# A gated layer's activation: ScalarE's silu in place of its sigmoid and a VectorE product

## The chip, the cores and the metric

The kernel runs on one core of one Trainium2 chip. The metric is the device time of one execution in microseconds (us), the median of several runs. The core has a matrix engine (TensorE, PE in the profile, with its weight loads as PEld), a vector engine (VectorE, DVE), an activation engine (ScalarE, ACT), GpSimd (POOL), and SyncE (SP), which here only issues transfers. Matmul results land in PSUM, which has 8 banks of 128 x 512 fp32.

## The reference

Four layers run over `x` of 8 x 512 x 512 fp32, each as `x = x + layernorm(layer(layernorm(x)))`: a softmax attention of `x` with itself, a mixing by a sum of eight factors, a grouped-query attention, and a gated feed-forward layer. The last is the one that matters here:

```python
g = jnp.einsum('th,ih->ti', xf, gate_w) * gate_s
u = jnp.einsum('th,ih->ti', xf, up_w) * up_s
hdn = jax.nn.silu(g) * u
out = jnp.einsum('ti,hi->th', hdn, down_w) * down_s
```

The hidden size is 512 and the inner size 1408, which is 11 blocks of 128. `silu(g)` is `g * sigmoid(g)`. The weights `gate_w`, `up_w` and `down_w` hold only -1, 0 and 1.

## The kernel before

The kernel works through eight batches of 512 tokens, each held as four tiles of 128 tokens by 512. For each batch it runs four stages: `stage_attn0`, `stage_ffn0`, `stage_attn1` and `stage_ffn1`. They are not executed in the order of the code. Every operation is first recorded by `Recorder.add` (line 75) with its engine, an estimated duration, the buffers it reads and writes, and a priority. The priority comes from a table of due times by kind of step and batch (`DUE`, line 1285, and `due`, line 1348). After all operations of all batches are recorded, `Recorder.issue` (line 118) goes through an estimated time line. At each step it looks, for each engine, at the operations that are ready and for which buffers are free. Among those that can start within a small slack of the earliest it takes the one that is due first, and then issues the pick that starts earliest over all engines. Each engine executes its instructions in the order so found. One batch's softmax rows and layernorms thus come to lie between the matmuls of another batch. The estimates count a change of the activation table on ACT as 1.3 us, and changes between shapes of the matmul array on PE as 0.09 or 0.21 us.

Buffers are handed out in the same pass: a `row` buffer (18 of them) holds a 128 x 512 tile in SBUF, `f` is one of the eight PSUM banks, `wgu` one of four buffers for a block of gate or up weights, `hd0` and `hd1` hold the hidden activations of a batch, `hl` (two) the split operands of a matmul.

The last layer is `stage_ffn1`. Its matmuls run in a reduced fp32 format on operands that are split into a leading part and a rest (`in_parts`, line 1083: ACT writes the leading part at line 1094, DVE the rest at 1103). For each of the 11 blocks of the inner size it

- loads a block of gate weights and one of up weights by `load_slice`, on POOL's queue (line 382),
- multiplies the gate block with the tokens into bank `pg` and the up block into bank `pu`, 8 matmuls each (line 1160),
- applies the sigmoid on ACT with the per-row scale `gate_s` (line 1180), from `pg` into a `row` buffer `sig`,
- forms `pg * gate_s * sig` on DVE, in place in `sig` (line 1190),
- forms `pu * up_s * sig` on DVE into `hd` (line 1199).

When all blocks are there, the down matmuls (line 1228) multiply `hd` with the resident `wd`, and line 1249 scales the result and hands it to the layernorm and the residual sum (lines 511 to 554).

In all but the last batch a gate block covers the 512 tokens at once. In the last batch the first four blocks (`FEW`) are done for tokens 0 to 255 and then for 256 to 511, so that there are 92 gate products in all: 84 of 128 x 512 and 8 of 128 x 256.

Two readings of other lines are needed below. Line 575 is the softmax exponential, the only other function that needs a table of its own; its maxima are taken on DVE at line 568. Lines 608, 658, 865, 885, 900, 922, 982 and 1014 are copies and scalings on ACT that bring results out of PSUM.

The whole program is recorded twice, the second time in plain fp32 behind a condition that the data of this case does not meet. Line 240 reads the flag for it.

Of the kernel before, what the change touches and what calls it, by code (L numbers as in the profile page):

```python
# [13 lines left out]
AF = mybir.ActivationFunctionType  # L14
ALU = mybir.AluOpType
# [235 lines left out]
def layers(  # L251
# [23 lines left out]
    nc = tc.nc  # L275
# [67 lines left out]
    add = rec.add  # L343

    def when(kind, b, *steps):

        rec.prio = due(kind, b if b < B // 2 else b - B, B, *steps)
# [23 lines left out]
    gs = Fixed("gs", [P, NI])  # L371
# [124 lines left out]
    def ap(r):  # L496
        return r[1](buf_of(r).t)

    def whole(b):
        return (b, lambda t: t[:, :])  # L500
# [609 lines left out]
    def stage_ffn1(x, b, after):  # L1110
        PASS, array = (0.229, "128x128r") if split else (0.86, "128x128")
        xs = [Buf("hl") for _ in range(1 + split)]
        hds = [Buf(f"hd{c}") for c in range(len(CUTS))]


        every = tuple(range(NT))
        rounds, kind = [(every, range(NI))], "f1."
        if b in EARLY or b - B in EARLY:
            rounds = [((0, 1), range(FEW)), ((2, 3), range(FEW)), (every, range(FEW, NI))]
            kind = "h1."  # L1120
        known, products, rows = set(), [], []
        for q, (toks, its) in enumerate(rounds):
            cut = slice(toks[0] * P, (toks[-1] + 1) * P)
            mine = [(x_, (t, hf)) for x_ in xs for t in toks for hf in range(2)]
            took = (0.69, 0.75) if len(toks) == NT else (0.4, 0.42)
            for t in toks:
                if t in known:
                    continue
                known.add(t)
                when(kind + "norm", b, t - toks[0], q)  # L1130
                if t % 2 == 0:
                    pair = [Buf("row"), Buf("row")]
                xn = pair[t % 2]
                mv, rstd = moments(whole(x[t]))
                normalize(whole(xn), whole(x[t]), mv, rstd, room=[*xs, *pair])
                rows.append(whole(xn))
                if t % 2 == 0:
                    continue
                pts, into, bank = transpose_two(xs[0], t - 1, rows[-2:], room=xs, copy=False)
                for hf in range(2):  # L1140
                    dsts = [((x_, (t, hf)), into(hf)) for x_ in xs]
                    in_parts(dsts, lambda hf=hf, bank=bank: bank(hf), [pts[hf]], 0.6, also=(t - 1, hf))

            for c, (lo, hi) in enumerate(CUTS):
                for it in range(lo, hi):
                    if it not in its:
                        continue
                    when(kind + "gate", b, it, q)
                    sig = Buf("row")
                    hd = (hds[c], lambda tt, k=it - lo, cut=cut: tt[:, k, cut])  # L1150
                    pg, pu = Buf("f"), Buf("f")
                    wg = load_slice("wgu", gate_t, it, after=after)
                    wu = load_slice("wgu", up_t, it, after=after)

                    def product(bank, w, cut=cut):
                        def go():
                            n = 0
                            for kt in range(KT):
                                for d in xs:
                                    nc.tensor.matmul(  # L1160
                                        bank.t[:, cut],
                                        w.t[:, kt, :],
                                        d.t[:, kt, cut],
                                        start=(n == 0),
                                        stop=(n == KT * len(xs) - 1),
                                    )
                                    n += 1

                        return go


                    us = PASS * KT * len(xs) * len(toks) / NT
                    mm(pg, us, product(pg, wg), [wg, *mine], room=[hds[c]], state=array)
                    products.append(mm(pu, us, product(pu, wu), [wu, *mine], state=array))
                    gsc = lambda it=it: gs.t[:, it : it + 1]
                    usc = lambda it=it: us_.t[:, it : it + 1]
                    add(
                        "ACT",
                        took[0],
                        lambda sig=sig, pg=pg, gsc=gsc, cut=cut: nc.scalar.activation(  # L1180
                            sig.t[:, cut], pg.t[:, cut], AF.Sigmoid, scale=gsc()
                        ),
                        reads=[pg, gs],
                        writes=[sig],
                        state="sig",
                    )
                    add(
                        "DVE",
                        took[1],
                        lambda sig=sig, pg=pg, gsc=gsc, cut=cut: nc.vector.scalar_tensor_tensor(  # L1190
                            sig.t[:, cut], pg.t[:, cut], gsc(), sig.t[:, cut], ALU.mult, ALU.mult
                        ),
                        reads=[pg, gs],
                        writes=[sig],
                    )
                    add(
                        "DVE",
                        took[1],
                        lambda sig=sig, pu=pu, usc=usc, hd=hd, cut=cut: nc.vector.scalar_tensor_tensor(  # L1199
                            ap(hd), pu.t[:, cut], usc(), sig.t[:, cut], ALU.mult, ALU.mult  # L1200
                        ),
                        reads=[pu, us_, sig],
                        writes=[(hds[c], (it - lo, u)) for u in range(2) if 2 * u in toks],
                    )
        for t in range(NT):
            po = Buf("f")
            for c, (lo, hi) in enumerate(CUTS):
                when(kind + "down", b, t, c)
                n = hi - lo
                if split:  # L1210

                    hl = Buf("hl")
                    half_of = lambda k, hl=hl, n=n: (
                        (hl, k),
                        lambda tt, k=k, n=n: flat(tt)[:, k * KT * D // 2 :][
                            :, : n * P
                        ].rearrange("p (i q) -> p i q", q=P),
                    )
                    src = lambda c=c, t=t: hds[c].t[:, :, ts(t, P)]
                    in_parts([half_of(0), half_of(1)], src, [(hds[c], (k, t // 2)) for k in range(n)], 0.78)  # L1220
                    ops = [half_of(0), half_of(1)]
                else:
                    ops = [(hds[c], lambda tt, t=t: tt[:, :, ts(t, P)])]

                def down(ops=ops, po=po, lo=lo, hi=hi):
                    for it in range(lo, hi):
                        for k, o in enumerate(ops):
                            nc.tensor.matmul(  # L1228
                                po.t[:, :],
                                ap(o)[:, it - lo, :],  # L1230
                                wd.t[:, it, :],
                                start=(it == 0 and k == 0),
                                stop=(it == NI - 1 and k == len(ops) - 1),
                            )

                add(
                    "PE",
                    PASS * n * len(ops),
                    down,
                    reads=[*{buf_of(o): 0 for o in ops}, wd],  # L1240
                    writes=[po],
                    after=products,
                    state=array,
                )
            z = Buf("row")
            add(
                "DVE",
                0.69,
                lambda po=po, z=z: nc.vector.tensor_tensor(
                    z.t[:, :], po.t[:, :], ds_bc.t[:, :], ALU.mult  # L1250
                ),
                reads=[po, ds_bc],
                writes=[z],
            )
            add_layernorm(whole(x[t]), whole(z), last=b == B - 1)
            add(
                "SP",
                0.85,
                lambda t=t: nc.sync.dma_start(out[b, ts(t, P), :], x[t].t[:, :]),
                reads=[x[t]],  # L1260
            )
# [138 lines left out]
```

## Time and profile before

| what | us |
|---|---|
| time, median of 3 runs (lowest to highest) | 1484.42 (1483.66 to 1485.83) |
| span of the profiled execution, first to last instruction | 1482.8 |
| PE busy in it | 1441.2 |
| DVE busy | 1059.0 |
| ACT busy | 624.6 |
| POOL busy | 570.3 |
| sigmoid, line 1180: 92 instructions | 61.7 |
| product with the gate, line 1190: 92 instructions | 66.7 |
| product with the up part, line 1199: 92 instructions | 66.4 |
| activation table loads: 16 of 1.283 us | 20.5 |

A line of a group in the profile reads: line of the kernel, engine, operation, output and input by the program's names, partitions x elements, the count, then busy us and the mean ns of one, and last the engine's idle time just before these instructions with what ended most of it (`<-`). A line of a wait reads: who waited for whom, then us in total, how many times, and the longest. The slices cut the span in 40 equal parts; a digit is the busy share in tenths. Matmuls are pipelined, so that PE's busy time is not work at its peak rate.

### The profile page before, as it was taken

The numbers are of one execution on the slowest core, as the hardware profiler recorded it, in microseconds if no ns is written. First come the engines' busy times: TensorE is split into PE (matmuls) and PEld (weight loads), VectorE is DVE, ScalarE is ACT, GpSimd is POOL, SyncE is SP. The second block draws the span as 40 slices with busy tenths as digits, with TensorE's granted clock in tenths as the row PEclk, the third lists the DMA queues.
The fourth block names the chain that finished last, engine by engine and source line by source line (L and its number), as shares of the span: only waits on it lengthen the run. The fifth ranks groups of instructions, "written<-read, shape, count | busy, mean of one in ns | idle before, by whom it ended". The sixth has DMA issues, their size and how long they took to land.

```text
span 1482.8 us, 23191 instructions
## 1 busy us (share of the span) xinstructions
PE 1441.2 (97%) x8562; PEld 906.9 (61%) x8562; DVE 1059.0 (71%) x2227; ACT 624.6 (42%) x1396; POOL 570.3 (38%) x884
## 2 busy tenths in 40 slices
PE   5999999999999999999999999999999999999986
PEld 3545567665756567565675656656566565765675
DVE  6989875778558784777838777487774868658745
ACT  3217534732257222672227712376114751247321
POOL 7760452137501473006720167201761117600541
PEclk9999999999999999999999999999999999999999
DMA  9632145014500254002540035300442003510281
GB/s 332 186 90 96 45 87 97 26 40 100 107 25 20 43 112 87 29 16 50 114 79 29 23 80 100 64 23 29 105 80 51 30 23 78 111 25 23 60 165 35
DMA packets 156700, 108.06 MB, mean 73 GB/s; under 512 B 7072, under 2 KB 137120, under 8 KB 156576
## 3 DMA queue, kind: packets, MB, share of 16 engines
q0 software_dynamic: 98736, 51.13, 18.4%
q1 hardware_dynamic: 57840, 55.34, 12.1%
q8 instruction: 70, 1.15, 0.3%
q14 instruction: 54, 0.44, 0.1%
HBM read 98.06 MB, written 8.39 MB: 72 GB/s over the span
## 4 chain that ended last, share of the span: by engine, by line
PE 78%; POOL 9%; DVE 8%; issue 2%; DMA 2%; SPq 0%; ACT 0%; POOLq 0%; DVEq 0%; ACTq 0%
PE f L1160 18%; PE f L1228 9%; PE f L939 8%; PE f L1001 8%; PE f L910 7%; PE f L1027 7%; PE f L970 5%; PE f L741 4%; PE f L688 4%; POOL rstd L527 3%; DVE row L535 3%; PE f L719 2%; PE f L880 2%; PE f L891 2%; DVE st L511 2%
## 5 line engine op out<-in xcount | busy, mean ns | idle before, releaser
L1160 PE MATMUL f<-hl,wgu 128*128 128x512 f32 (+1 forms) x1472 | 347.8, 391 | 6.1 <-DMA wgu<-in_up_t 3.0
L520 POOL TENSOR_SCALAR ve<-mv 128x1 f32<-128x1 f32 x224 | 67.6, 302 | 724.3 <-DVE mv L516 711.7
L1160 PEld LDWEIGHTS f<-hl,wgu 128*128 128x128 f32 x1472 | 265.9, 188 | 71.7 <-issue 14.4
L575 ACT ACTIVATE row<-f,s 128x512 f32<-128x512 f32 x288 | 196.7, 696 | 34.6 <-DVE s L568 31.9
L568 DVE TENSOR_REDUCE s<-f 128x1 f32<-128x512 f32 x288 | 185.5, 683 | 30.3 <-PE f L939 18.5
L1228 PE MATMUL f<-wd,hl 128*128 128x512 f32 x704 | 185.4, 415 | 1.4 <-DVE hl L1103 1.4
L554 POOL TENSOR_TENSOR x<-x,row 128x512 f32<-128x512 f32 x120 | 156.1, 1305 | 67.0 <-DVE row L535 62.0
L1180 ACT ACTIVATE row<-f,gs 128x512 f32<-128x512 f32 (+1 forms) x92 | 61.7, 670 | 243.9 <-PE f L1160 239.6
L1228 PEld LDWEIGHTS f<-wd,hl 128*128 128x128 f32 x704 | 131.9, 188 | 45.5 <-issue 9.7
L592 DVE TENSOR_SCALAR row<-row,s 128x512 f32<-128x512 f32 x288 | 147.7, 517 | 8.6
L982 ACT COPY big<-f 128x512 f32<-128x512 f32 x256 | 134.8, 598 | 40.3 <-PE f L970 37.9
L527 POOL TENSOR_TENSOR rstd<-ve,mhalf 128x1 f32<-128x1 f32 x224 | 135.2, 606 | 16.5
L939 PE MATMUL f<-row,big 64*128 64x512 f32 x512 | 128.7, 610 | 0.0
L1190 DVE SCALAR_TENSOR_TENSOR row<-f,gs,row 128x512 f32<-128x512 f32 (+1 forms) x92 | 66.7, 725 | 79.0 <-ACT row L1180 79.0
L1001 PE MATMUL f<-big,row 128*64 128x256 f32 x1024 | 120.4, 383 | 0.0
L1199 DVE SCALAR_TENSOR_TENSOR hd<-f,us,row 128x512 f32<-128x512 f32 (+1 forms) x92 | 66.4, 722 | 73.7 <-PE f L1160 71.7
L910 PE MATMUL f<-big,row 128*128 128x512 f32 x256 | 117.1, 601 | 0.0
L719 PE MATMUL f<-big,big 128*128 128x512 f32 x256 | 114.6, 597 | 1.1 <-DVE row L535 1.1
L741 PE MATMUL f<-fsum,row 128*128 128x512 f32 x256 | 115.5, 594 | 0.2 <-ACT row L575 0.2
L1027 PE MATMUL f<-row,big 128*128 128x512 f32 x256 | 114.9, 599 | 0.0
L1001 PEld LDWEIGHTS f<-big,row 128*64 128x64 f32 x1024 | 69.5, 137 | 51.3 <-ACT big L982 15.3
L970 PEld LDWEIGHTS f<-ident,row 64*128 64x128 f32 x2048 | 73.4, 139 | 40.6 <-issue 20.4
(84 smaller groups left out, 1849.2 us busy)
## 6 DMA issues: line engine op xcount, KB each, us to landing
wgu<-in_gate_t POOLq DMA_DIRECT2D x92, 256.0 KB, 3.5
wgu<-in_up_t POOLq DMA_DIRECT2D x92, 256.0 KB, 3.4
x<-in_x SPq DMA_DIRECT2D x32, 256.0 KB, 2.7
row<-in_wq_t SPq DMA_DIRECT2D x32, 256.0 KB, 5.0
row<-in_wo_t SPq DMA_DIRECT2D x32, 256.0 KB, 3.1
out<-x SPq DMA_DIRECT2D x32, 256.0 KB, 2.0
hd<-in_factors SPq DMA_DIRECT2D x28, 256.0 KB, 4.9
wd<-in_down_t POOLq DMA_DIRECT2D x11, 256.0 KB, 8.6
```

Source lines behind the costliest of these rows:

```text
L527: lambda: nc.gpsimd.tensor_tensor(rstd.t[:, :], ve.t[:, :], mhalf, ALU.pow),
L554: lambda: on.tensor_tensor(ap(xt), ap(xt), y.t[:, :], ALU.add),
L568: lambda: nc.vector.tensor_reduce(nmax.t[:, :], sc.t[:, :], AX.X, ALU.max, negate=True),
L575: lambda: nc.scalar.activation(e.t[:, :], sc.t[:, :], AF.Exp, bias=nmax.t[:, :], accum_out=tot.t[:, :]),
L592: lambda: nc.vector.tensor_scalar(e.t[:, :], e.t[:, :], rtot.t[:, :], None, ALU.mult),
L741: nc.tensor.matmul(po.t[:, :], xnT.t[:, ts(kt, P)], fsum.t[:, kt, :], start=(kt == 0), stop=(kt == KT - 1),)
L910: nc.tensor.matmul(pq.t[:, :], wq.t[:, ts(kt, P)], hT.t[:, kt, :], start=(kt == 0), stop=(kt == KT - 1),)
L939: nc.tensor.matmul(scs[g].t[:, :], qT.t[gp, i, ts(s, P)], kT.t[gp, :], start=True, stop=True,)
L1001: nc.tensor.matmul(po.t[gp, : 2 * P], v.t[:, t * P + g * DH : t * P + (g + 1) * DH], columns_of(aT)[:, g * NT + t, :], start=(t == 0), sto ...
L1027: nc.tensor.matmul(po.t[:, :], qT.t[:, i, ts(t, P)], wos[i].t[:, :], start=(i == 0), stop=(i == NPAIR - 1),)
L1160: nc.tensor.matmul(bank.t[:, cut], w.t[:, kt, :], d.t[:, kt, cut], start=(n == 0), stop=(n == KT * len(xs) - 1),)
L1228: nc.tensor.matmul(po.t[:, :], ap(o)[:, it - lo, :], wd.t[:, it, :], start=(it == 0 and k == 0), stop=(it == NI - 1 and k == len(ops) - 1),)
```

## The change

The activation on ACT becomes `Silu` with the same operands, the same estimated duration and the same table state `"sig"` for the planner. The DVE operation at line 1190 is no longer recorded. Line 1199 reads `sig` as before; what it reads there is now written by ACT alone. Bank `pg` has one reader less. Nothing else differs in the source: the estimates, due times and buffers stay.

```diff
@@ -1178,20 +1178,11 @@
                         "ACT",
                         took[0],
                         lambda sig=sig, pg=pg, gsc=gsc, cut=cut: nc.scalar.activation(
-                            sig.t[:, cut], pg.t[:, cut], AF.Sigmoid, scale=gsc()
+                            sig.t[:, cut], pg.t[:, cut], AF.Silu, scale=gsc()
                         ),
                         reads=[pg, gs],
                         writes=[sig],
                         state="sig",
-                    )
-                    add(
-                        "DVE",
-                        took[1],
-                        lambda sig=sig, pg=pg, gsc=gsc, cut=cut: nc.vector.scalar_tensor_tensor(
-                            sig.t[:, cut], pg.t[:, cut], gsc(), sig.t[:, cut], ALU.mult, ALU.mult
-                        ),
-                        reads=[pg, gs],
-                        writes=[sig],
                     )
                     add(
                         "DVE",
```

## The prediction

> **What bounds the kernel now.** I read the profile's totals and slices first, then the stretches of time, then what TensorE (PE) waited for, and last the instructions of the changed lines.
>
> ```profile
> span 1482.8 us, 23191 instructions
> ...
> PE 1441.2 (97%) x8562; PEld 906.9 (61%) x8562; DVE 1059.0 (71%) x2227; ACT 624.6 (42%) x1396; POOL 570.3 (38%) x884
> ...
> PE   5999999999999999999999999999999999999986
> ```
>
> PE is busy 1441.2 of 1482.8 us. Only 41.6 us exist in which it does nothing, whatever the other engines do. The stretches (start:end, length, busy time of each engine) show where those 41.6 us lie:
>
> ```profile
> 0.00:50.00 50.00, 33.74 (x180) 18.94 (x181) 35.40 (x72) 13.90 (x30) 34.22 (x60) 1.00 0.99 322
> 50.00:93.00 43.00, 38.92 (x185) 19.95 (x184) 39.53 (x84) 11.43 (x31) 33.86 (x50) 1.00 0.33 92
> 93.00:205.00 112.00, 110.91 (x732) 59.71 (x732) 100.59 (x220) 55.58 (x138) 42.35 (x62) 0.98 0.30 85
> ...
> 385.00:565.00 180.00, 179.57 (x1069) 113.02 (x1068) 127.14 (x273) 78.19 (x175) 67.72 (x107) 1.00 0.27 59
> ...
> 1395.00:1424.00 29.00, 23.96 (x158) 18.81 (x157) 18.76 (x37) 6.72 (x13) 16.21 (x24) 1.00 0.68 129
> ```
>
> The start costs 16.3 + 4.1 + 1.1 = 21.5 us, and the first instruction of a changed line comes at 213.3 us, so that part stays. A batch in the middle (about 180 us) leaves PE idle for 0.43 us. From 1395 to 1424 us it is idle for 5.0 us, later for 1.6 us more, and 10 us of layernorm and store follow its last matmul. VectorE (DVE) is 71% busy and no bound: 127 of 180 us in a middle batch. What PE waited for, with total us, times, longest:
>
> ```profile
> PE f L1160 <- DMA wgu<-in_up_t: 3.0, 3, 1.5
> ...
> PE f L604 <- DVE row L535: 2.3, 8, 0.6
> ...
> PE f L719 <- DVE row L535: 1.1, 5, 0.2
> PE f L1160 <- DMA wgu<-in_gate_t: 1.1, 2, 0.8
> PE f L1160 <- DVE row L1190: 0.8, 1, 0.8
> ```
>
> The product that is removed, L1190, held PE up once, for 0.8 us. The others here are weights that land late (4.1 us) and normalized rows that come late (3.4 us).
>
> **The change part by part.** The three groups of the gate (busy us, mean ns, then the engine's idle time before them):
>
> ```profile
> L1180 ACT ACTIVATE row<-f,gs 128x512 f32<-128x512 f32 (+1 forms) x92 | 61.7, 670 | 243.9 <-PE f L1160 239.6
> ...
> L1190 DVE SCALAR_TENSOR_TENSOR row<-f,gs,row 128x512 f32<-128x512 f32 (+1 forms) x92 | 66.7, 725 | 79.0 <-ACT row L1180 79.0
> ...
> L1199 DVE SCALAR_TENSOR_TENSOR hd<-f,us,row 128x512 f32<-128x512 f32 (+1 forms) x92 | 66.4, 722 | 73.7 <-PE f L1160 71.7
> ```
>
> *The product removed.* 92 instructions at 725 ns are 66.7 us of DVE, 8.2 us in a middle batch (11 at 750 ns). On the path to the end they are worth almost nothing, which the last product of the last batch shows, all engines in order of time (start, us, engine, line):
>
> ```profile
> 1447.92 2.43 PE L1160 MATMUL f<-hl,wgu 128*128 128x512 f32 x10
> ...
> 1448.57 0.69 ACT L1180 ACTIVATE row<-f,gs 128x512 f32<-128x512 f32 x1 [2.94 <-PE f L1160]
> ...
> 1449.29 0.75 DVE L1190 SCALAR_TENSOR_TENSOR row<-f,gs,row 128x512 f32<-128x512 f32 x1 [1.79 <-ACT row L1180]
> ...
> 1450.38 0.75 DVE L1199 SCALAR_TENSOR_TENSOR hd<-f,us,row 128x512 f32<-128x512 f32 x1 [0.34 <-PE f L1160]
> ```
>
> L1190 ends at 1450.04, and L1199 starts only at 1450.38, when PE has finished the up product. The up matmuls (8 at some 0.227 us, 1.81 us) cover the sigmoid (0.69) and L1190 (0.75) with 0.34 us over. Without L1190 the cover is about 1.1 us and L1199 still starts when the up product ends: 0 us. If that cover were gone, 0.75 us would be saved once per product, 66.7 us of DVE at most, and still not of PE.
>
> *The wait.* L1199 waits for ScalarE (ACT) directly. DVE's 79.0 us of idle time before L1190 moves in front of L1199, where PE ends it. Queued behind L1199 are softmax maxima (L568) and layernorm steps (L511, L535) of the other batch; they are not held longer, because L1199 itself is released by the same event as before. The queue of loads for the weights (POOL) and SP's stores are issued on releases by PE and POOL; none of these instructions is moved.
>
> *The bank of the gate product* is released by ACT's end instead of L1190's, 0.8 us earlier (1449.26 against 1450.04). That takes away the wait of 0.8 us at 1410 us. The products around it wait 0.7 to 1.5 us each for weights, so I count half: -0.4 us, bounds 0 and -0.8.
>
> *DVE work that comes earlier.* PE's waits for L535 total 3.4 us in the two rows above, 0.1 to 0.6 us each. With DVE lighter some vanish: bounds 0 and -3.4, taken -0.5, since these waits lie mostly after a layernorm chain through POOL and not behind an L1190.
>
> *The function.* Silu isn't in the trace. The nearest row is the sigmoid with the same operands, 689 ns for 128x512; the plain copy of that size takes 598 (L982) and the exponential 696 plus 209 for its accumulator. Bounds 598 to 905 ns, -8.4 to +19.9 us of ACT over 92 instructions. I take 689: +0. ACT is 78 of 180 us busy in a middle batch; even 905 ns ends about 0.9 us before the up product. 0 us on the path, at both ends.
>
> *Table loads.* There are 8 in front of the sigmoid, 7 in front of the exponential:
>
> ```profile
> L1180 ACT ACT_TABLE_LOAD x8 | 10.3, 1283 | 24.0 <-issue 18.6 <-PE f L1160 5.4
> L575 ACT ACT_TABLE_LOAD x7 | 9.0, 1283 | 5.6 <-DVE s L568 5.6
> ```
>
> Copies run between sigmoids without a load. If silu's table serves copies too, the count stays at 16 and the price is 0. If not, each change costs a load of 1.28 us; copies break into the run of sigmoids some 4 times in a middle batch, 8 loads more, 10 us of ACT, which has 100 us free there.
> The Trainium skill ("ScalarE: Activation LUTs", What ACT_TABLE_LOAD costs) speaks against mixing functions: it puts a switch at 2.66 us, drain included. Here the sigmoid follows a load of 1.283 us by 0.02 us (212.04 + 1.28, next start 213.34). By the skill's figure those 8 would be 21 us of ACT in a batch instead of 10, an estimate; either is hidden. The same page, Table sets, says that cheap functions such as copy are in every set, by which the count would not change at all; no run here shows that yet.
>
> *The order.* Every engine's order is computed from estimated durations, and with 92 entries gone from DVE's line it is computed anew. Up to about 212 us nothing differs; after that any decision may. The trace has no row for the new order, so I bound it by stretches of the old one. From 205 to 1395 us PE is idle for 3.6 us (0.3%), read from seven such stretches. Below: all of that gone, -3.6. Above: a stretch that is not the repeating pattern, 93 to 205 us, idles 1.09 of 112 us, 1.0%; over 1190 us that is 11.6 us, so +8.0. PE's order of array shapes matters as well: the same 8 matmuls of L910 take 3.44 us on the chain behind L891's and 3.63 us behind the 64-row ones of L939, 0.2 us for a change of shape. I counted 55 such changes between kinds in a middle batch, so one more or less in each is 0.2 x 6.6 batches = 1.3 us. I take +2.0, nearer to the repeating rows, since the work is the same and DVE, which feeds PE, is lighter.
>
> *Sum.* -0.4 - 0.5 + 0 + 0 + 2.0 = +1.1 us. The profiled execution has a span of 1482.8 us; the median of the three runs is 1484.42, 1.6 us more, for what lies around the span. 1482.8 + 1.6 + 1.1 = 1485.5 us.
>
> **The rivals.** *No change* (my forecast): PE is as full as before, within 3 us, which is 0.2% and about what the runs can tell.
>
> *Slower: the new order starves PE.* Place: PE's queue between 212 and 1395 us, where softmax rows, transposes and layernorms of one batch fill in between the products of the other. Price: the 1.0% of the stretch at 93 to 205 us, +8.0 us: 1484.4 + 8.0 = 1492.4 us. It decides from 0.45 us more idle (or two to three more changes of shape) in each of 6.6 batches, 3 us. For it: the pattern repeats from batch to batch, so one bad wait is paid about six times, and it has only 0.43 us of idle time now, so it can hardly get better and easily worse. Against: two batches overlap, and PE has ready work nearly always.
>
> *Faster: the new order closes gaps.* The idle 3.6 us in the middle and 5.0 us at 1395 to 1424 us are all that can be had there; half of both is -4.3: 1480.1 us. For it: L1190's wait lies in that last stretch, and DVE's layernorms stand there between L1190s. Against: most of that stretch is weights that land late, and their release is PE's, not DVE's.
>
> *The function doesn't come cheap:* a table without the copy and 905 ns. ACT would go from 78 to about 91 of 180 us (11 x 0.216 + 8 x 1.28 more); only where PE waits for a copy at once would a load show, say 2 of the 8 in a batch, 2 x 1.28 x 6.6 = 17 us: 1501 us. Against: tables that hold the sigmoid hold the copy as well.
>
> **How the numbers follow.** No change 0.42, slower by the order 0.36, faster 0.19, the function dear 0.03. The time is the first's, 1485.5, whose own range is 1481.4 to 1487.4. To hold 8 in 10 the range goes down to the faster case's middle, 1480, and up past the slower one's, 1495. By sign: faster 0.19, same 0.42, slower 0.36 + 0.03 = 0.39.
>
> **What the next profile would show.** DVE near 992 us in all (1059.0 - 66.7); ACT near 625; 16 table loads; silu at 689 ns; L1199 waiting for PE; no PE wait for the gate's bank; PE busy within 3 us of 1441. A middle batch with PE idle for over 0.9 us, or a larger loss at 1395 to 1424 us, means the order's rival. I am wrong about the path if the span falls by over 5 us: then PE waited for DVE in ways its wait list does not show.

## The result and the profile after

Over 20 runs of each, the changed kernel takes 1486.87 us (1485.29 to 1487.84) and the kernel before 1484.34 us (1483.34 to 1486.28). The ratio is 1.0016, 95% interval 1.0009 to 1.0022: 2.5 us slower, which is just resolved and smaller than 0.2%. 66.7 us of VectorE work are gone and nothing is won.

The totals of the profile after, the slowest of its 20 runs (1487.84 us):

```profile
span 1486.0 us, 23145 instructions
...
PE 1447.9 (97%) x8562; PEld 909.0 (61%) x8562; DVE 1000.1 (67%) x2135; ACT 624.1 (42%) x1396; POOL 569.1 (38%) x884
```

DVE has 92 instructions less and is 58.9 us less busy, not the 66.7 us of its products; where the other 7.8 us went was not traced. PE, with exactly the same 8562 matmuls, is 6.7 us *more* busy: 4.2 us of it in the 7460 matmuls from the first of line 1160 on, 2.4 us ahead of them. Its idle time is 38.1 us, 3.5 us less than before. That is the first thing to see: PE waits less and still ends later. The stretches after (start:end, length, busy time of PE, PEld, DVE, ACT and POOL, then PE's granted clock and the transfers):

```profile
93.00:205.00 112.00, 110.47 (x716) 59.40 (x718) 99.61 (x219) 54.70 (x137) 42.77 (x62) 0.97 0.30 85
205.00:385.00 180.00, 179.58 (x1079) 119.27 (x1076) 118.87 (x254) 78.49 (x170) 69.90 (x108) 1.00 0.32 68
385.00:565.00 180.00, 180.00 (x1058) 110.99 (x1057) 124.12 (x269) 77.56 (x174) 69.67 (x111) 1.00 0.24 56
565.00:745.00 180.00, 178.98 (x1069) 113.93 (x1068) 115.85 (x251) 78.00 (x174) 64.84 (x103) 1.00 0.28 62
745.00:925.00 180.00, 180.00 (x1057) 111.17 (x1057) 123.73 (x269) 77.69 (x174) 70.28 (x111) 1.00 0.24 56
925.00:1105.00 180.00, 178.99 (x1069) 113.92 (x1068) 115.86 (x251) 77.99 (x174) 64.85 (x103) 1.00 0.28 62
```

Before, every middle batch repeated the one ahead of it. After, the pattern repeats only every second batch (DVE 124.1, 115.9, 123.7, 115.9), which can't come from removing an instruction alone: the order is another one. The first stretch has to be set apart. There PE's clock is 0.97 instead of 0.98: the profile records a piece at half clock (0.5 granted) near 93 us, which lasted 6.8 us in this execution and 3.4 us in the one before. The first matmul of line 1160 comes at 210.26 instead of 208.55 us. Going by the starts of the same matmuls, 0.4 us of these 1.7 us were there before that piece and 1.3 us came with it. These 1.7 us of the 3.2 us between the two spans belong to the executions and not to the change: up to that point PE's order is the same. From the first matmul of line 1160 to the last matmul of all it is 1263.97 us before and 1265.63 us after. I use this length below, as it leaves the start out.

The wait list of PE after:

```profile
PE f L604 <- DVE row L535: 2.8, 5, 0.8
...
PE f L1160 <- DMA wgu<-in_gate_t: 2.4, 4, 0.8
PE f L1219 <- DVE hl L1103: 1.5, 1, 1.5
...
PE f L1160 <- DMA wgu<-in_up_t: 0.8, 2, 0.6
PE f L719 <- DVE row L535: 0.6, 3, 0.2
```

The wait for L1190 is gone, and the waits for weights are 3.2 instead of 4.1 us. The waits after 205 us add up to 7.6 us, where before they were 10.2 us.

The groups of the gate, where line 1190 is now the product with the up part, and the table loads:

```profile
L1190 DVE SCALAR_TENSOR_TENSOR hd<-f,us,row 128x512 f32<-128x512 f32 (+1 forms) x92 | 66.6, 725 | 169.2 <-PE f L1160 165.2 <-ACT row L1180 4.0
...
L1180 ACT ACTIVATE row<-f,gs 128x512 f32<-128x512 f32 (+1 forms) x92 | 61.6, 670 | 228.8 <-PE f L1160 227.5 <-DVE s L850 1.2
...
L1180 ACT ACT_TABLE_LOAD x8 | 10.3, 1283 | 15.2 <-issue 11.1 <-PE f L1160 4.1
...
L575 ACT ACT_TABLE_LOAD x7 | 9.0, 1283 | 0.1
...
L658 ACT ACT_TABLE_LOAD x1 | 1.3, 1283 | 0.7 <-PEq L1377 0.7
```

Silu has the sigmoid's mean to the ns, and the 16 table loads are still 16. DVE's product now waits 165.2 us for PE and 4.0 us for ACT. The last product of the last batch, in order of time:

```profile
1451.00 2.65 PE L1160 MATMUL f<-hl,wgu 128*128 128x512 f32 x11
...
1451.88 0.69 ACT L1180 ACTIVATE row<-f,gs 128x512 f32<-128x512 f32 x1 [2.94 <-PE f L1160]
...
1453.76 0.75 DVE L1190 SCALAR_TENSOR_TENSOR hd<-f,us,row 128x512 f32<-128x512 f32 x1 [2.88 <-PE f L1160]
```

From silu's start to the start of the product with the up part it is 1.88 us; before it was 1.81 us (1448.57 to 1450.38) with a whole DVE instruction in between. Silu's result has been there for 1.2 us when the product starts.

### The profile page after: what moved, and what is told of

It reads as the page before. It is cut to its first block, busy times and chain, and to the rows that moved or that the text cites. A ratio compares the mean times of both kernels' runs of the same rounds, so it can differ in the third digit from the quotient of the medians.

```text
span 1486.0 us, 23145 instructions
## 1 busy us (share of the span) xinstructions
PE 1447.9 (97%) x8562; PEld 909.0 (61%) x8562; DVE 1000.1 (67%) x2135; ACT 624.1 (42%) x1396; POOL 569.1 (38%) x884
## 4 chain that ended last, share of the span: by engine, by line
PE 84%; DVE 6%; POOL 6%; issue 2%; DMA 1%; SPq 0%; ACT 0%; POOLq 0%; DVEq 0%
PE f L1160 20%; PE f L1219 10%; PE f L939 8%; PE f L1001 8%; PE f L910 7%; PE f L1027 6%; PE f L741 6%; PE f L970 5%; PE f L688 4%; PE f L719 4%; DVE row L535 2%; POOL rstd L527 2%; PE f L630 2%; PE f L880 2%; PE f L891 2%
## 5 line engine op out<-in xcount | busy, mean ns | idle before, releaser
L1190 DVE SCALAR_TENSOR_TENSOR hd<-f,us,row 128x512 f32<-128x512 f32 (+1 forms) x92 | 66.6, 725 | 169.2 <-PE f L1160 165.2
L592 DVE TENSOR_SCALAR row<-row,s 128x512 f32<-128x512 f32 x288 | 150.8, 527 | 9.0
L719 PE MATMUL f<-big,big 128*128 128x512 f32 x256 | 114.8, 598 | 0.6 <-DVE row L535 0.6
L382 POOL DMA_DIRECT2D wgu<-in_gate_t x92 | 72.7, 790 | 76.7 <-PE f L1160 71.8
```

The lines of the kernel that those rows point to most:

```text
L719: nc.tensor.matmul(po.t[:, :], xnT.t[:, j, ts(t, P)], wT.t[:, j, :], start=(j == 0), stop=(j == KT - 1),)
```

## The experiments

All were compared with runs of the kernel before on the same chip. "Changes of shape" are changes between matmuls that use the array at full height and width (the fp32 and the reduced fp32 ones) and those on 64 rows or 64 columns (lines 630, 939, 970, 1001), counted along PE's order up to the end. "Length" is that from the first matmul of line 1160 to the last of all, from one profile each. "Waits" are PE's after 205 us by its wait list, which leaves short pauses out; in runs 7 and 8, 3.1 us of them lie ahead of the length. Changes between 64 rows and 64 columns are not counted. From the first matmul of line 1160 on there are 64 of them in the kernel before and in runs 1, 5 and 6, 73 in the change's order, 69 in run 9, 83 in run 10.

| kernel | median us | ratio to before, 95% interval | changes of shape | length us | waits us |
|---|---|---|---|---|---|
| before | 1484.34 | | 177 | 1263.97 | 10.2 |
| the change | 1486.87 | 1.0016 (1.0009 to 1.0022) | 197 | 1265.63 | 7.6 |
| 1 silu, order of before | 1484.08 | 0.9997 (0.9988 to 1.0006) | 177 | 1263.19 | 9.2 |
| 2 new order, late product | 1491.35 | 1.0045 (1.0032 to 1.0059) | 197 | 1271.25 | 10.0 |
| 3 sigmoid alone | 1487.33 | 1.0018 (1.0009 to 1.0027) | 197 | 1265.87 | 7.9 |
| 4 new order, early product | 1494.61 | 1.0066 (1.0052 to 1.0079) | 197 | 1274.24 | 14.1 |
| 5 thirty changes more | 1501.12 | 1.0112 (1.0097 to 1.0127) | 207 | 1278.04 | 17.0 |
| 6 twenty changes more | 1489.81 | 1.0034 (1.0022 to 1.0046) | 197 | 1268.86 | 9.5 |
| 7 silu, other due times | 1488.85 | 1.0027 (1.0018 to 1.0037) | 179 | 1263.68 | 13.9 |
| 8 product, the due times of 7 | 1485.77 | 1.0011 (1.0002 to 1.0020) | 179 | 1259.80 | 10.3 |
| 9 silu, due times, same start | 1485.14 | 1.0002 (0.9993 to 1.0011) | 171 | 1263.84 | 10.5 |
| 10 product, the due times of 9 | 1498.62 | 1.0087 (1.0074 to 1.0101) | 201 | 1278.81 | 15.4 |

(Runs 5 and 6 are run 1 with 30 and 20 changes of shape put in.)

**1. Silu in the order of before.** The planner still counts the product, but nothing is issued for it, so that every engine keeps its order and only the product is missing:

```diff
                     add(
                         "DVE",
                         took[1],
-                        lambda sig=sig, pg=pg, gsc=gsc, cut=cut: nc.vector.scalar_tensor_tensor(
-                            sig.t[:, cut], pg.t[:, cut], gsc(), sig.t[:, cut], ALU.mult, ALU.mult
-                        ),
+                        lambda: None,
                         reads=[pg, gs],
                         writes=[sig],
                     )
```

> Silu as in the change, but the planner still counts 0.75 us of DVE for the product, for which nothing is issued: every engine keeps the order of the kernel before, only the 92 products are gone (184 with the part that is not executed). Theory (the order costs the time): back to the kernel before or a little under it, 1483.4 to 1484.6 us, 394 changes of array shape on PE as before, PE busy within 1 us of 1441. Rival (silu, or line 1199 waiting for ACT directly, costs the time): 1486 to 1487 us as with the change.

1484.08 us against 1484.82 of the kernel before: the same within the interval, 0.7 us less nominally. The extra time of the change is gone. So neither silu nor the direct wait for ACT costs anything; the order does. The stretches show how exactly everything else stands still, and what the product was worth:

```profile
565.00:745.00 180.00, 179.44 (x1066) 1.00 0.27 60
745.00:925.00 180.00, 179.27 (x1064) 1.00 0.27 60
...
1395.00:1424.00 29.00, 24.62 (x161) 1.00 0.72 136
```

The middle batches are those of before within 0.04 us (179.48 and 179.24 there; this view is of PE alone). The length is 0.78 us shorter, 0.5 us of it after 1400 us, where the wait of 0.8 us for L1190 lay; the other 0.3 us were gained at 1288 to 1291 us, in matmuls of line 1160, and why was not traced. PE's waits for normalized rows did not get shorter: L604 still waits 2.3 us for L535, as before.

**3. The sigmoid alone in the new order.** Only the function differs from the change; the kernel leaves out the product with the gate.

```diff
-                            sig.t[:, cut], pg.t[:, cut], AF.Silu, scale=gsc()
+                            sig.t[:, cut], pg.t[:, cut], AF.Sigmoid, scale=gsc()
```

> The change with the sigmoid in place of silu and no product: the same instructions in the same order, only the function differs (the product with the gate is left out). Theory: 1486.3 to 1487.5 us, ACTIVATE at 689 ns, 16 table loads of 1283 ns. Rival (silu is dearer than the sigmoid): under 1485.5 us.

1487.33 us, and a length of 1265.87 against 1265.63 us. The two functions cost the same.

**2 and 4. The product put back into the new order.** Run 2 issues a DVE product of the same shape together with the product with the up part (it multiplies by the up bank where the real one takes the gate bank), run 4 the real one with the sigmoid. The planner counts neither. Run 2, at line 1190 of the change:

```diff
-                        lambda sig=sig, pu=pu, usc=usc, hd=hd, cut=cut: nc.vector.scalar_tensor_tensor(
-                            ap(hd), pu.t[:, cut], usc(), sig.t[:, cut], ALU.mult, ALU.mult
+                        lambda sig=sig, gsc=gsc, pu=pu, usc=usc, hd=hd, cut=cut: (
+                            nc.vector.scalar_tensor_tensor(
+                                sig.t[:, cut], pu.t[:, cut], gsc(), sig.t[:, cut], ALU.mult, ALU.mult
+                            ),
+                            nc.vector.scalar_tensor_tensor(
+                                ap(hd), pu.t[:, cut], usc(), sig.t[:, cut], ALU.mult, ALU.mult
+                            ),
                         ),
```

Run 4, at line 1180:

```diff
-                        lambda sig=sig, pg=pg, gsc=gsc, cut=cut: nc.scalar.activation(
-                            sig.t[:, cut], pg.t[:, cut], AF.Silu, scale=gsc()
+                        lambda sig=sig, pg=pg, gsc=gsc, cut=cut: (
+                            nc.scalar.activation(
+                                sig.t[:, cut], pg.t[:, cut], AF.Sigmoid, scale=gsc()
+                            ),
+                            nc.vector.scalar_tensor_tensor(
+                                sig.t[:, cut], pg.t[:, cut], gsc(), sig.t[:, cut], ALU.mult, ALU.mult
+                            ),
                         ),
```

> The order of the change, with the sigmoid and with a DVE product of the same shape issued right ahead of each product with the up part (it reads the up bank in place of the gate bank, so that bank's release is the change's; the output is not the reference's). 66.7 us of DVE are back. Theory (DVE's product is off the path, the order alone costs): 1486 to 1488 us. Rival (the product's removal gained several us and the order lost more): 1489 us or over.

> The order of the change with the sigmoid and the real product of the kernel before, issued on DVE right behind each sigmoid (the planner doesn't count it). The second run put a product of the same shape late, next to the product with the up part, and took 1491.35 us. If DVE's load is what costs there: 1490 to 1492 us again. If it was the late place, which makes the hidden activations 0.75 us later: 1486.5 to 1488.5 us, near the change's own time.

1491.35 and 1494.61 us. Run 2's time lies in the range of the rival written down for it, whose reason (the removal gained several us) run 1 does not bear out; run 4's is over both of its ranges. The late place alone is not to blame, since the early one costs more. Here the product is not hidden. In run 4 DVE stands and waits for ACT with what is queued behind it (the first line), and PE waits for layernorm rows:

```profile
DVE row L1184 <- ACT row L1181: 120.5, 72, 8.8
...
PE f L604 <- DVE row L535: 6.2, 11, 1.7
PE f L630 <- DVE row L535: 3.5, 8, 0.9
```

With the change the two waits of PE were 2.8 and 1.5 us. The waits after 205 us are 6.5 us more than with the change, of 8.6 us in length; the other 2.1 us lie in PE's busy time, with PE's order unchanged, and were not traced. In run 2 the waits are 2.4 us more, and the profile holds 3.4 us of half clock at 1459 us, 1.7 us lost, of 5.6 us; 1.5 us stay open. That the product "is off the path" thus holds for an order that was made with it in the list. Taken out of that order it is worth 0.7 us; put into an order made without it, it costs 4.5 to 7.7 us.

**5 and 6. More changes of array shape, and nothing else.** These kernels take run 1 and, after the planner is done, put single matmul groups behind the next group on PE: two more changes of shape at each place.

```diff
-            op.fn()
+            seq.append(op)
...
+        if split:
+            pe = [op for op in seq if op.eng == "PE"]
+            for j in LATER:
+                seq.remove(pe[j])
+                seq.insert(seq.index(pe[j + 1]) + 1, pe[j])
+        for op in seq:
+            op.fn()
         return clock
...
+LATER = (155, 185, 230, 260, 290, 334, 364, 394, 438, 468, 498, 542, 572, 602, 646)
```

> Silu in the order of the kernel before (as in the first run), but at 15 places, three in each of five batches, a matmul group of full height is put behind the next one of 64 rows or columns. Each group runs at most one short group (0.6 to 0.9 us) later; changes between full height and 64 on PE go from 177 to 207, other changes from 217 to 212; all work is the same. The stretches of the change's trace where its waits are no longer put a change at 0.1 to 0.2 us. Theory (the new order costs by its changes of array shape): PE's time grows by 3 to 6 us, 1487 to 1490 us, with PE's waits as before. Rival (changes of shape are free, and the change's order costs by waits): 1483.5 to 1485 us.

1501.12 us, 17 us more than run 1. That is far over what I expected, because a third of the places also made PE wait: L638 for L543 (630 and 535 in the kernel before) 9.9 us in all against 1.7 us in run 1, one of 1.6 us in each of the five batches. The length grew by 14.85 us and the waits by 7.8 us, which leaves 7.05 us for 30 changes, 0.24 us each. Run 6 leaves those five places out (185, 290, 394, 498, 602):

> As the run with 30 more changes of array shape, but only ten of its fifteen places: left out are those behind which PE then waited 1.6 us a batch for a normalized row (8.2 us of that run's 15). Silu, the order of the kernel before, and 197 changes between full height and 64 in place of 177, which is also the count of the change's order (197). That run's time less its waits gives 1.2 us for six changes a batch, 0.2 us each. Theory (a change of shape costs 0.2 us): 20 x 0.2 = 4 us over the first run's 1484.1, 1487.5 to 1488.6 us, PE's waits as in the first run. Rival (those 1.2 us were waits that the list doesn't show): 1484 to 1486 us.

1489.81 us. Its waits are run 1's: the middle has these, 3.5 us in all against 3.3 us.

```profile
PE f L612 <- DVE row L543: 1.4, 6, 0.3
PE f L727 <- DVE row L543: 1.2, 5, 0.2
PE f L1168 <- DVE hl L1111: 0.7, 1, 0.7
PE f L638 <- DVE row L543: 0.2, 1, 0.2
```

The length grew by 5.68 us, 0.3 us of it waits: 0.27 us for each of 20 changes, somewhat over the 0.2 us that I had put down. One place can be read directly, in the chain of waits in order of time. First run 1, then run 6, the same matmuls (line 1226 there is 1234 here, 970 is 978):

```profile
461.67 5.13 PE f L1226 x22
466.80 1.64 PE f L970 x48
```

```profile
462.86 2.79 PE f L1234 x12
465.65 0.64 PE f L978 x16
466.29 2.52 PE f L1234 x10
468.81 1.14 PE f L978 x32
```

6.77 us have become 7.09 us, 0.16 us for each of the two added changes, and all of it counts as PE being busy. PE's busy time from the first matmul of line 1160 on shows the same: the kernel before, run 1, run 3, the change, run 6.

```profile
208.55:1473.00 1264.45, 1254.10 (x7460) 1.00 0.28 62
...
208.13:1473.00 1264.87, 1254.22 (x7460) 1.00 0.29 62
...
208.69:1476.00 1267.31, 1258.15 (x7460) 1.00 0.28 62
...
210.26:1477.00 1266.74, 1258.34 (x7460) 1.00 0.28 62
...
208.19:1478.00 1269.81, 1258.87 (x7460) 1.00 0.28 61
```

Run 1, in the order of before, needs what the kernel before needs; 20 changes more are 4.65 us more in run 6 (0.23 us each) and 4.1 us more with the change (0.21 us each). The change's order has 9 more changes between 64 rows and 64 columns as well, and if these cost too, the price of one is lower there; runs 5 and 6 add none of these. Measured from start to start of PE's matmuls without the waits, the change's trace has 7.5 us more than run 1's at the places where the shape changes (full, 64 rows and 64 columns taken as three), 3.1 us less where the line changes and the shape stays, and 0.2 us less elsewhere. The Trainium skill says in "TensorEngine Tiling (Array Packing)", Key Properties, that a change of the tiling mode drains the engine. The runs agree with it in that a change costs time: 0.16 us in that one place, 0.24 and 0.27 us in the mean of runs 5 and 6 by their waits. The drain itself is in no row.

**7 and 8. Other due times.** If only the order stands between the change and a gain, an order made for the shorter list should win. Due times were moved in small steps, and steps kept whose planned end came earlier. The planner's shifts by batch, its preference for staying with a shape (`STAY`) and its slack were moved with them. Run 7 has them with silu, run 8 with the sigmoid and the product. For example:

```diff
-    "f1.gate": (1.4467, 0.0118),
-    "f1.down": (1.6308, 0.297, 0.0562),
+    "f1.gate": (1.3303, 0.0162,),
+    "f1.down": (1.612, 0.3328, 0.0719,),
```

> The change with other due times, found by trying small steps of them and keeping those whose planned end came earlier; 179 changes between full height and 64 in place of 197. Theory (only the order stands between the change and its gain): under the kernel before, 1481 to 1484 us. Rival (silu has nothing to give on this path, and the order of the kernel before was as good as any): 1484 to 1487 us.

> The same other due times for the kernel before, with the sigmoid and the product, planned with them. If the product is hidden wherever the order is made for it: within 1.5 us of the run with silu and these due times. If silu's lighter DVE is what makes a better order possible: 3 us or more over it.

1488.85 and 1485.77 us: both theories of run 7 missed, and so did both of run 8, which with the product is the faster one by 3.1 us. The start went wrong: PE idles there as it did not before. Its busy time in the stretches, run 7, then run 8:

```profile
93.00:205.00 112.00, 108.21 (x694) 0.98 0.29 81
205.00:385.00 180.00, 175.88 (x1073) 0.99 0.30 64
```

```profile
93.00:205.00 112.00, 109.18 (x688) 0.97 0.29 81
205.00:385.00 180.00, 177.60 (x1089) 1.00 0.31 66
```

The first matmul of line 1160 comes at 216.7 and 214.0 us, where the others have it at 208 to 210 us. In both, PE waits 3.1 us for a normalized row just ahead of it (run 7, then run 8); why DVE is late with it was not traced:

```profile
208.12 1.32 PE L630 MATMUL f<-ident,row 64*128 64x64 f32 x32 [3.07 <-DVE row L535]
```

```profile
207.05 1.21 PE L630 MATMUL f<-ident,row 64*128 64x64 f32 x32 [3.08 <-DVE row L535]
```

Run 8's length, 1259.80 us, is 4.2 us shorter than that of the kernel before, *with* the product, and the run loses it all before 214 us.

**9 and 10. Due times with the start left alone.** As 7 and 8, but the due times of the first loads stay, and a change of shape has a price in the choice. In run 9 the first matmul of line 1160 comes at 208.6 us. For example:

```diff
-    "f1.gate": (1.4467, 0.0118),
-    "f1.down": (1.6308, 0.297, 0.0562),
+    "f1.gate": (1.488, 0.012,),
+    "f1.down": (1.674, 0.2864, 0.0268,),
```

> The change with due times found by small steps again, but with those that decide the first 200 us left alone (in the two runs with other due times the first product came 5 to 8 us later than in the kernel before) and with a price on changes of array shape: 171 between full height and 64, in place of 197 with the change and 177 with the order before. Theory (0.2 to 0.28 us for each, the product's removal itself worth 0.7): 6 x 0.2 to 0.28 = 1.2 to 1.7 us under the first run's 1484.1, 1482.2 to 1483.2 us, and under both kernels. Rival (other waits come with a new order, as in most): 1484 to 1488 us.

> The kernel before, sigmoid and product, with the due times of the other run of this pair, which were found without the product: the change the other way round. Its order has 201 changes between full height and 64 in place of 177. Theory (a list of due times fits one list of operations, and either edit spoils it): 24 x 0.2 to 0.28 = 5 to 7 us over the kernel before, 1489 to 1492 us. Rival (the lighter DVE of silu is what matters): within 2 us of the other run of the pair.

Run 9 has 171 changes of shape and takes 1485.14 us, the same as the kernel before and not under run 1. Less its waits its length is 0.7 us under run 1's, half of what I expected of six changes less, and the waits are 1.3 us more (L630 and L719 for L535), which takes it back. Its 5 more changes between 64 rows and 64 columns may be why the six won so little. Run 10 is the change turned round: due times found without the product, and the product in the list. It takes 1498.62 us, 13.5 us over the kernel before, more than I expected. Its length is 14.84 us over that of the kernel before: 5.2 us of waits, 10.2 us at half clock, in which PE worked for 7.9 us and so lost 4.0 us, and 5.6 us that remain for 24 changes of shape, 0.23 us each (and for 19 more between 64 rows and 64 columns). Two waits for split operands (`hl`) stand close together at the end:

```profile
1410.19 0.38 PE L1160 MATMUL f<-hl,wgu 128*128 128x256 f32 x1 [1.16 <-ACT hl L1094]
1415.40 1.86 PE L1160 MATMUL f<-hl,wgu 128*128 128x256 f32 x7 [4.83 <-DVE hl L1103]
```

PE stood for 4.8 us, and over the stretch from 1395 to 1424 us its granted clock was 0.88. Whether the first of these waits brought the second was not tried.

No version beat the kernel before by more than the runs can tell. Run 1 comes nearest, with 0.9997 (0.9988 to 1.0006).

## Why the prediction was right, and where it was right by luck

The measured time lies in the forecast's own range, 1485.5 us forecast and 1486.87 us measured, and the terms were these. They add up to +1.1 us; the lengths show +1.66 us and the medians +2.5 us.

- *The product removed, 0 us on the path.* Right for the order it stood in: run 1 is 0.78 us shorter, and 0.5 us of that lie where the bank's wait below was. I had said that even without that cover the product would not be time of PE; runs 2 and 4 show that in another order the same 66.7 us cost 4.5 and 7.7 us.
- *The bank of the gate product, -0.4 us.* Right: the wait of 0.8 us is gone from run 1, and the length after 1400 us is 0.5 us shorter; waits for weights beside it took back the rest, as the term had it.
- *DVE work that comes earlier, -0.5 us.* Not seen. In run 1, where nothing else changed, the waits of L604 and L719 for L535 are 2.3 and 1.0 us against 2.3 and 1.1 us. The bound of 3.4 us was too wide as well: 0.9 us of it lie ahead of 205 us, where nothing changes.
- *The wait of line 1199.* Right: its release is PE's in 165.2 of 169.2 us.
- *The function and the table loads, 0 us.* Right: 670 ns mean in both, 16 loads in both, run 3 equal to the change. The rule of the Trainium skill that speaks for it, in "ScalarE: Activation LUTs", Table sets (copy is in every set), agrees with the loads counted here. The drain with which the same page, What ACT_TABLE_LOAD costs, comes to 2.66 us a switch did not appear as a gap: the first silu starts at 215.0 us, right behind the load that starts at 213.7 us and takes 1.283 us, and ACT had been idle for 0.02 us ahead of that load.
- *The order, +2.0 us.* From run 1 to the change it is +2.44 us in length, so the size was near, by luck. The composition was not. I had chosen a point between bounds made of PE's idle time, and the rival beside it was that PE starves; but PE waits 1.6 us less than in run 1. The cost is the one that I named in passing at 0.2 us a change and valued at 1.3 us, one change a batch: it was 20 more changes of shape, three a batch (the rival's "two to three more changes of shape", not its idle time), which leave 2.44 + 1.6 = 4.0 us, 0.20 us each, near the 0.23 to 0.27 us of runs 5, 6 and 10.
- *The signs.* PE busy within 3 us of 1441: missed, 1447.9 us, of which 2.4 us belong to the start. DVE near 992 us: 1000.1. PE idle for over 0.9 us in a middle batch, which was to mean the order's rival, came in every second batch (1.0 us) with 0.0 us between, so that two batches together are idle for 1.0 us, as against 0.95 and 1.19 us before; and the loss at 1395 to 1424 us shrank from 5.0 to 3.1 us. By that sign alone one would have blamed waits.

The first place where the two orders of PE differ can be found. PE, before and after:

```profile
376.95 7.87 PE L1160 MATMUL f<-hl,wgu 128*128 128x512 f32 x32
384.66 0.60 PE L604 MATMUL f<-ident,row 128*128 128x128 f32 x4
```

```profile
378.61 9.69 PE L1160 MATMUL f<-hl,wgu 128*128 128x512 f32 x40
388.13 0.60 PE L604 MATMUL f<-ident,row 128*128 128x128 f32 x4
```

DVE, freed of the products, takes the product with the up part ahead of a layernorm's moments (line 781) at 375.4 us, where before it took the moments first. A fifth gate or up product of 1.8 us then goes ahead of the transposes of line 604. From there on everything is shifted, and from the next batch on the pattern has a period of two batches, with 8 more changes of shape in each such period (48 against 40). That this one decision is the cause of the period was not tried.

## What to carry to other kernels

Where a program writes out the order from a list of operations and their estimates, removing one operation is two edits: the work that goes, and a new order for all that stays. Measure them apart by leaving a placeholder in the list; here the work was worth some 0.7 us and the new order cost 2.4 us by the lengths and 2.8 us by the medians. And if the busiest engine gets busier with the same instructions, count its changes of shape before looking for waits, since here what they cost was counted as busy time.

## What was not expected of the hardware

The half clock that the profiles record comes in pieces of 3.4 or 6.8 us while PE works. Near 93 us it is 3.4 us long in most profiles, 6.8 us in that of the change and of run 8, and missing in runs 9 and 10. A piece costs PE about half of its length: without it, runs 9 and 10 gain 1.7 us on the kernel before by 100 us. They don't keep it, since PE then waits for a softmax row where it did not before (run 9; it is 1.5 us in run 10 too):

```profile
112.83 3.70 PE L910 MATMUL f<-big,row 128*128 128x512 f32 x8 [1.51 <-ACT row L575]
```

So one piece there is nearly free, and the second one in the change's profile costs 1.3 us, half of what the change costs. The lengths agree with the Trainium skill, "TensorE: Matmul & The Clock Gate", What's actually happening, which has a free-running window of 3413 ns. Further pieces appear at 1459 us in run 2, at 28, 209 and 1424 us in run 7, at 1413 (6.8 us, from the middle of the wait of 4.8 us on) and 1437 us in run 10. Long waits in all don't bring them by themselves: runs 4 and 5, with 14.1 and 17.0 us, have none between 97 us and PE's last matmul.
